# Output product of the first half moved up two slots in the first SAGE pass of a two-layer graph network

## The chip, the cores and the metric

The kernel runs on one core of a Trainium2 chip. The metric is the device time of one execution in microseconds; the time given for a kernel is the median over its runs. Engines of the core are written as in the profile: PE is TensorE (PEld its weight load), DVE is VectorE, ACT is ScalarE, POOL is GpSimd, SP is SyncE, which here only issues DMAs. Each engine works through its own instructions in the order in which the program gives them.

## The reference

Sixteen graphs of 1024 nodes with 128 channels go through two layers. Layer 0 is a gated graph network of four steps. Layer 1 thins out the adjacency row by row (`_dilate`), then runs three SAGE layers, each with a batch norm over all graphs, and a closing linear layer; each of the two layers ends with a residual sum and a layer norm. The part that matters here is the first SAGE layer:

```python
def _sage(x, adj, Wr, Wx, b, mf):
    deg = jnp.clip(jnp.sum(adj, axis=-1, keepdims=True), 1.0, None)
    agg = jnp.einsum('bij,bjd->bid', adj, x) / deg
    out = agg @ Wr + x @ Wx + b
    nrm = jnp.maximum(jnp.linalg.norm(out, axis=-1, keepdims=True), NORM_EPS)
    return out / nrm * mf[..., None]
...
h1 = _bn(jax.nn.relu(_sage(x, adj_d, Wr1, Wx1, b1, mf)), g1, be1)
h2 = _bn(jax.nn.relu(_sage(h1, adj_d, Wr2, Wx2, b2, mf)), g2, be2)
```

## The kernel before

The program has a stage for layer 0 and the thinning (up to about 1284 us of the profile), then `Sage.first` (to about 1747 us), `Sage.second`, `Sage.third` and `Sage.last`. The change lies in `Sage.first` alone.

`first` goes through the graphs b = -1 to 15, and through 16 slots t for each (`slot`, L1609). In a slot two things are interleaved: work on graph b (`now`), and preparation of the next graph n = b + 1 (`nxt`). The order in which `slot` issues instructions is the order on each engine; nothing is reordered by a scheduler there (`manual_schedule` over all engines).

Preparation of n: the transposed adjacency of the thinned graph is built in 16 units, one per slot. `unit` (L1482) issues four matmuls with the identity into a PSUM tile `p_u`, of which there are two, and an ACT instruction (L1495) for the part above the diagonal; `unit_low` (L1498) is one DVE instruction (L1503) for the part below it, and reads `p_u` too. `pack` (L1506) turns a finished unit into bytes on POOL a slot later. Units 3 to 7 have no ACT part, units 8 to 11 no DVE part. x of the next graph is normed (`norm_stats`, `norm`), turned by PE and copied by ACT into `p_xt0` and `p_xt1` (`turn_x`), and split into a high and a low part (`split_x`: ACT cast L1419, POOL subtraction L1420), `p_xh` and `p_xl`.

Work on b, with f = 0, 1 for the two halves of 512 nodes:

- the sum over neighbours: eight matmuls on `p_xh` (high sum) and eight on `p_xl` (low sum) into one PSUM bank, slots 0 and 1 for f = 0, slots 3 and 4 for f = 1 (`agg`, L1568);
- its copy to SBUF by ACT (`evict`, L1573, tile `s_ag`) at the head of slots 2 and 5, then the degrees (`degrees`: DVE L1556, ACT cast L1557 into `p_row`), whose columns PE turns in slots 3 and 6 (`degree_columns`, L1559; DVE L1565 and L1566);
- the output product (`out_first`, L1579): twelve matmuls into `p_oa` (aggregate by Wr) and `p_ob` (bias parts and x by Wx), each of one PSUM buffer;
- the chain of the half: `scale_rows` (DVE L1395, L1396), `squares` (ACT L1403 eight records, L1404), `rows` (DVE L1409 to L1414), `split_r` (ACT L1419, POOL L1420) into `p_rh` and `p_rl`;
- the neighbour sums of r for the second SAGE layer on `p_rh` and `p_rl` in slots 9, 10, 12 and 14, both halves of columns in one slot, and the turn of r in slots 11 and 13 (`turn_r`).

`check` (L1513) is a DVE instruction over a loaded block of the adjacency in slots 2, 5, 8, 10, 12 and 14. Between PE's instructions of one slot the order is: unit, sum, output product, degree columns, turn of r, sum of r, turn of x. In one slot, slot 6, `unit_low` is issued behind `scale_rows` rather than right after the unit.

SP's queue takes, in program order, the loads of the next adjacency blocks (`load_a`), of the thinning's result (`load_nr`) and of x, and the stores: bytes of the adjacency, the three rows of `rho` (L1690, slot 7), r (L1692), x (L1697), and in slot 1 the sums of r of the graph before (L1708), which frees the two buffers of `s_ag`. POOL issues no DMA in this pass.

In graph 0, the weights are prepared at the end of slot 3 (`first_weights`, L1306): it replaces the first row of `wr[:, 0, :]`, fills the bias rows `r6`, and fills the node mask.

Of the kernel before, what the change touches and what calls it, by code (L numbers as in the profile page):

```python
# [917 lines left out]
class Gated:  # L918
# [25 lines left out]
    def bank(self):  # L944
        return self.ps6.tile([P, HF], F32, name="h_g")
# [264 lines left out]
class Sage:  # L1210
# [398 lines left out]
    def slot(self, b, t):  # L1609

        nc, g, n = self.nc, self.g.get(b), b + 1
        now, nxt = b >= 0, n < B

        if nxt:
            if t in (4, 6):
                self.load_nr(n + 1, (t - 4) // 2)
            if t == 7:
                self.load_s(n + 1)
            if t in (10, 13):
                self.load_a(n, 2 + t // 13)  # L1620
        if now and t in (0, 2, 5, 8):
            self.load_a(b, (0, 2, 5, 8).index(t) + 4)

        if now:
            if t in (2, 5):
                g["ag", t // 5] = self.evict(g.pop(("pa", t // 5)), -1, 0)
            if t == 15:
                g["ag2"] = [self.evict(g.pop(("pb", f)), b, f) for f in range(2)]
        if nxt:
            self.unit(n, t)  # L1630
            if t != 6 or not now:
                self.unit_low(n, t)
            if t:
                self.pack(n, t - 1)
        if now and t == 0:
            self.pack(b, 15)
        if now:
            bank = lambda: self.ps3.tile([C, HF], F32, name="p_ag")
            if t in (2, 5):
                self.degrees(b, t // 5)  # L1640
            if t in (0, 1, 3, 4):
                f, lo = t // 3, t in (1, 4)
                if not lo:
                    g["pa", f] = bank()
                self.agg(g["pa", f], (self.xh, self.xl)[lo], g["at"], f, range(NB), not lo, lo)
            if t in (5, 7):
                self.out_first(b, t // 7)
            if t in (6, 8):
                f = t // 8
                g["o", f] = self.scale_rows(b, f, g.pop(("oa", f)), g.pop(("ob", f)))  # L1650
                if t == 6 and nxt:
                    self.unit_low(n, t)
            if t in (3, 6):
                pt = bank() if t == 6 else self.ps1.tile([P, 4, P], F32, name="s_tr").rearrange("p a b -> p (a b)")
                self.degree_columns(b, t // 6, pt[:, :4])
            if t in (7, 9):
                f = t // 9
                g["r", f] = self.rows(b, f, g.pop(("o", f)), g.pop(("ss", f)))
            if t in (8, 10):
                self.split_r(b, t // 10)  # L1660
            if t in (6, 8):
                g["ss", t // 8] = self.squares(g["o", t // 8])
            if t in (11, 13):
                self.turn_r(0, b, t // 13, self.ps1)
            if t in (9, 10, 12, 14):
                part = g["rl"] if t in (10, 14) else g["rh"]
                js = range(4 * (t // 12), 4 * (t // 12) + 4)
                for f in range(2):
                    if t == 9:
                        g["pb", f] = bank()  # L1670
                    self.agg(g["pb", f], part, g["at"], f, js, t == 9, t == 14)

        if nxt:
            if t < 2:
                self.norm_stats(n, t)
            if t in (2, 3):
                self.norm(n, t - 2)
            if t in (6, 8):
                self.turn_x(n, t // 8)
            if t in (7, 12):  # L1680
                self.split_x(n, t // 12)
        if now and t in (2, 5, 8, 10, 12, 14):
            self.check(b, (2, 5, 8, 10, 12, 14).index(t) + 2)

        if now:
            if t == 2:
                nc.sync.dma_start(self.at8[b, 1], g["b", 1])
            if t == 7:
                for i in range(3):
                    nc.sync.dma_start(self.rho[b, i:i + 1, :], g["rho"])  # L1690
            if t in (13, 15):
                nc.sync.dma_start(self.rt[b, t // 15], g["rt", t // 15])  # L1692
        if nxt:
            if t == 10:
                nc.sync.dma_start(self.at8[n, 0], self.g[n]["b", 0])
            if t == 13:
                nc.sync.dma_start(self.x1[n], self.g[n]["s"])  # L1697
        if (b, t) == (-1, 11):
            self.load_given()
        if (b, t) == (-1, 15):  # L1700

            for i in range(3):
                nc.sync.dma_start(self.rho[:, 3 + i, :], self.mask48[:B, :])
        if (b, t) == (0, 3):
            self.first_weights()
        if t == 1 and b >= 1:
            for f in range(2):
                nc.sync.dma_start(self.ag[b - 1, f], self.g[b - 1]["ag2"][f])  # L1708
            del self.g[b - 1]
# [368 lines left out]
```

## Time and profile before

| what | value |
|---|---|
| median of 3 runs | 2189.92 us (2189.5 to 2190.53) |
| the profiled execution, whole | 2193.03 us |
| its span, first to last instruction | 2191.1 us |
| mean granted TensorE clock | 0.986 |
| first sum product of graph 1, of graph 15 | 1333.83 us, 1721.84 us |

The busy shares, engine by engine, hold for the whole span, over stages that have different limits. For this change the stretch of the 14 graphs between the last two times is what is to be read; one graph looks like the next there. The stretch by windows (busy us of each engine, number of instructions, granted clock, busy share of the DMA engines, GB/s):

```profile
1333.83:1721.84 388.01, 361.94 (x2688) 293.31 (x2686) 342.81 (x869) 251.97 (x715) 284.13 (x281) 1.00 0.86 297
```

The engines in that line are PE, PEld, DVE, ACT, POOL. In a timeline line the columns are the start, the time taken, the engine, the line, the operation, the tiles written and read, the shapes, how many instructions are merged, and in brackets the idle time just before with what ended it. A matmul of fp32 operands has two records, so eight records are four matmuls. The time taken of a group of matmuls is longer than the distance to the next group, since they are pipelined.

### The profile page before, as it was taken

How to read it: one execution, taken by the hardware profiler on the slowest of the kernel's cores; microseconds unless marked ns; L12 is line 12 of the kernel's file. 1: busy time of each engine (PE TensorE's matmuls, PEld its weight loads, DVE VectorE, ACT ScalarE, POOL GpSimd, SP SyncE). 2: the span in 40 equal slices, each digit the busy share in tenths (PEclk: the TensorE clock that was granted, in tenths of full speed). 3: DMA queues.
4: the chain of work that ended last, by engine and by line, in shares of the span. 5: the costliest groups of instructions: out<-in, count | busy, mean ns of one | idle time of the engine just before them, and what ended most of it. 6: DMA issues, size and time to landing. Idle time of an engine off the chain costs nothing. (4 is left out here: it accounts for less than half of the span.)

```text
span 2191.1 us, 32979 instructions
## 1 busy us (share of the span) xinstructions
PE 2068.8 (94%) x10217; PEld 1441.4 (66%) x10217; DVE 1838.4 (84%) x4215; ACT 1326.7 (61%) x3238; POOL 1240.4 (57%) x1226
## 2 busy tenths in 40 slices
PE   6999999999999999999999979999999899998977
PEld 4666556666556665556665557777777678887866
DVE  4898998989998889988989978888888767766878
ACT  3657557565666656656575566666666445555757
POOL 4458558467566476575585447777777445551002
PEclk9999999999999999999999989999999999999989
DMA  8348446456455276474383259888888577765505
GB/s 256 76 96 252 90 121 224 86 154 192 92 177 166 77 205 146 97 226 109 83 261 92 68 200 334 306 301 304 302 306 298 178 268 264 268 230 175 156 21 156
DMA packets 233853, 406.13 MB, mean 185 GB/s; under 512 B 79042, under 2 KB 100196, under 8 KB 233668
## 3 DMA queue, kind: packets, MB, share of 16 engines
q1 hardware_dynamic: 187844, 284.37, 39.9%
q0 software_dynamic: 41472, 117.46, 20.2%
q10 hardware_dynamic: 4352, 2.11, 0.4%
q8 instruction: 83, 1.36, 0.3%
q14 instruction: 102, 0.84, 0.1%
HBM read 313.48 MB, written 109.25 MB: 193 GB/s over the span
## 5 line engine op out<-in xcount | busy, mean ns | idle before, releaser
L1104 PE MATMUL h_g<-h_h,h_wh 128*128 128x512 f32 x768 | 396.0, 597 | 3.3 <-DVE h_r L1116 3.3
L1104 PE MATMUL h_g<-h_ms,h_wi 128*128 128x512 f32 x768 | 392.2, 592 | 0.0
L1123 POOL TENSOR_TENSOR h_zh<-h_r,h_h 128x512 f32<-128x512 f32 x126 | 175.4, 1392 | 258.9 <-ACT h_r L1119 255.8
L737 DVE TENSOR_TENSOR_SCAN f_rank<-f_a,f_first,f_pd 128x1024 f16<-128x1024 bf16 x128 | 299.4, 2345 | 4.2
L1092 PE MATMUL h_g<-h_a,h_hi 128*128 128x512 f32 x1024 | 278.8, 413 | 1.3 <-DMA h_a<-in_adj_dram 1.2
L1104 PEld LDWEIGHTS h_g<-h_ms,h_wi 128*128 128x128 f32 x768 | 145.5, 190 | 184.3 <-issue 169.4
L1511 POOL CAST p_b<-p_at 128x512 uint8<-128x512 f32 x256 | 219.7, 880 | 82.8 <-DVE p_at L1503 52.3
L1092 PE MATMUL h_g<-h_a,h_lo 128*128 128x512 f32 x1024 | 262.0, 393 | 0.2 <-DVE h_lo L1030 0.2
L1092 PEld LDWEIGHTS h_g<-h_a,h_hi 128*128 128x128 f32 x1024 | 190.1, 188 | 62.2 <-issue 21.8
L1403 ACT ACTIVATE s_junk<-s_o 128x128 bf16<-128x128 f32 x384 | 114.0, 298 | 169.2 <-DVE s_o L1396 158.3
L1092 PEld LDWEIGHTS h_g<-h_a,h_lo 128*128 128x128 f32 x1024 | 189.7, 188 | 39.0 <-DVE h_lo L1030 1.0
L1104 PEld LDWEIGHTS h_g<-h_h,h_wh 128*128 128x128 f32 x768 | 133.3, 190 | 100.3 <-issue 73.4
L1125 POOL TENSOR_TENSOR h_h<-h_h,h_zh 128x512 f32<-128x512 f32 x126 | 179.0, 1420 | 9.9
L1119 ACT ACTIVATE h_r<-h_r,h_bi 128x512 f32<-128x512 f32 x128 | 92.4, 722 | 151.5 <-DVE h_r L1118 151.4
L1124 POOL TENSOR_TENSOR h_zh<-h_z,h_zh 128x512 f32<-128x512 f32 x126 | 162.5, 1290 | 9.9
L1095 ACT COPY h_ms<-h_g 128x512 f32<-128x512 f32 x128 | 73.9, 577 | 149.7 <-PE h_g L1092 149.6
L910 ACT ACTIVATE f_u<-f_rank,f_q 128x128 f16<-128x128 f16 (+7 forms) x128 | 110.6, 867 | 69.4 <-DVE f_rank L850 69.4
L1778 PE MATMUL q_ob<-s_wxp,q_xt 128*128 128x256 f32 x512 | 125.3, 389 | 3.5 <-DVE s_ss L1409 2.1
L1992 DVE SCALAR_TENSOR_TENSOR p_junk<-p_a 128x1024 bf16<-128x1024 f32 x96 | 126.0, 1312 | 0.0
L887 ACT ACTIVATE f_pd<-f_rank,f_q 128x128 f32<-128x128 f16 x128 | 59.1, 462 | 98.7 <-DVE f_q L701 95.5
L1503 DVE SCALAR_TENSOR_TENSOR p_at<-p_nr,p_u 128x128 fp32r<-128x128 bf16 (+1 forms) x192 | 102.0, 543 | 18.0 <-ACT p_at L1495 14.6
L778 POOL TENSOR_SCALAR_AFFINE_SELECT f_both<-f_both 128x512 bf16<-128x512 bf16 x32 | 20.5, 642 | 165.1 <-DVE f_both L777 165.1
(264 smaller groups left out, 4807.8 us busy)
## 6 DMA issues: line engine op xcount, KB each, us to landing
h_a<-in_adj_dram POOLq DMA_DIRECT2D x128, 512.0 KB, 9.2
p_a<-in_adj_dram SPq DMA_DIRECT2D x96, 512.0 KB
f_a<-in_adj_dram POOLq DMA_DIRECT2D x128, 256.0 KB, 6.5
e_nr<-f_nr SPq DMA_DIRECT2D x128, 256.0 KB
p_nr<-e_nr SPq DMA_DIRECT2D x32, 1024.0 KB
h_test<-in_adj_dram SPq DMA_DIRECT2D x32, 512.0 KB
s_at<-p_b SPq DMA_DIRECT2D x32, 512.0 KB
s_ag<-s_ag SPq DMA_DIRECT2D x64, 256.0 KB
```

The costliest lines, as they stand in the source:

```text
L737: nc.vector.tensor_tensor_scan(out, a, other[:, 0, 0:1].to_broadcast([P, N]), start, op0=ALU.add, op1=ALU.bypass)
L910: nc.scalar.activation(u[:, :n1], rank[:, g, :n1], AF.Abs, bias=q[:, 1, g:g + 1], scale=q[:, 0, g:g + 1])
L1092: nc.tensor.matmul(pm[f], part[:, j, :], st.adj[j][:, half[f]], start=(j == 0 and n == 0), stop=(j == NB - 1 and n == 1))
L1104: nc.tensor.matmul(pg, lhs, rhs, start=(i == 0), stop=(i == len(mm) - 1))
L1123: aid.tensor_tensor(d, r, h, ALU.subtract)
L1124: aid.tensor_tensor(d, z, d, ALU.mult)
L1125: aid.tensor_tensor(h, h, d, ALU.add)
L1403: self.nc.scalar.activation(junk, o[:, i, :], AF.Square, accum_out=ss[:, i:i + 1])
L1503: self.nc.vector.scalar_tensor_tensor(g["at"][:, j, c0:c0 + low], v[:, j, c0:c0 + low], 0.0, pu[:, :low], op0=ALU.is_lt, op1=ALU.is_lt)
L1511: self.nc.gpsimd.tensor_copy(g["b", f][:, j, :], g["at"][:, j, f * HF:(f + 1) * HF].bitcast(F32))
L1778: nc.tensor.matmul(pb[:, i], g["xt"][:, f, blk], self.wxp, start=(i % 2 == 0), stop=False)
L1992: nc.vector.scalar_tensor_tensor(junk, a, 0.0, a, op0=ALU.is_gt, op1=ALU.not_equal, accum_out=bad[:, c:c + 1])
```

## The change

The output product of half 0 goes to slot 3, and the high sum of half 1 to slot 2, so the product stands between the high and the low sum of half 1. The chain of half 0 follows (`scale_rows` and `squares` in slot 4, `rows` in 6, `split_r` in 7). The output product of half 1 goes to slot 6, its `scale_rows` and `squares` to slot 7. `rows` and `split_r` of half 1 stay in 9 and 10. `turn_x` of half 0 goes to slot 5, `split_x` of half 0 to slot 8. `unit_low` is issued behind `scale_rows` in slots 4 and 7, no longer in slot 6. `first_weights` stays at the end of slot 3 of graph 0.

```diff
-            if t != 6 or not now:
+            if t not in (4, 7) or not now:
                 self.unit_low(n, t)
...
-            if t in (0, 1, 3, 4):
-                f, lo = t // 3, t in (1, 4)
+            if t in (0, 1, 2, 4):
+                f, lo = t // 2 if t < 4 else 1, t in (1, 4)
                 if not lo:
                     g["pa", f] = bank()
                 self.agg(g["pa", f], (self.xh, self.xl)[lo], g["at"], f, range(NB), not lo, lo)
-            if t in (5, 7):
-                self.out_first(b, t // 7)
-            if t in (6, 8):
-                f = t // 8
+            if t in (3, 6):
+                self.out_first(b, t // 6)
+            if t in (4, 7):
+                f = t // 7
                 g["o", f] = self.scale_rows(b, f, g.pop(("oa", f)), g.pop(("ob", f)))
-                if t == 6 and nxt:
+                if nxt:
                     self.unit_low(n, t)
...
-            if t in (7, 9):
+            if t in (6, 9):
                 f = t // 9
                 g["r", f] = self.rows(b, f, g.pop(("o", f)), g.pop(("ss", f)))
-            if t in (8, 10):
+            if t in (7, 10):
                 self.split_r(b, t // 10)
-            if t in (6, 8):
-                g["ss", t // 8] = self.squares(g["o", t // 8])
+            if t in (4, 7):
+                g["ss", t // 7] = self.squares(g["o", t // 7])
...
-            if t in (6, 8):
+            if t in (5, 8):
                 self.turn_x(n, t // 8)
-            if t in (7, 12):
+            if t in (8, 12):
                 self.split_x(n, t // 12)
```

## The prediction

> **What bounds the kernel now.** I read the share of busy time first, then the waits of the first SAGE pass (1290 to 1730 us), then one graph of it engine by engine in the timeline, then the granted clock by windows. The page's chain of waits names only the last ACT instruction, so the chain is followed by hand.
>
> ```profile
> PE 2068.8 (94%) x10217; PEld 1441.4 (66%) x10217; DVE 1838.4 (84%) x4215; ACT 1326.7 (61%) x3238; POOL 1240.4 (57%) x1226
> ```
>
> PE is busiest, but DVE is close behind. In the pass itself, from 1333.83 to 1721.84 us, PE is busy 361.94 and DVE 342.81 of 388.01 us. Those two times are the starts of the first product on p_xh in graphs 1 and 15, so a graph takes 388.01 / 14 = 27.72 us. PE's waits there, by their sums over 15 graphs:
>
> ```profile
> PE p_ag L1570 <- POOL p_rl L1420: 12.5, 15, 0.9
> PE p_ag L1570 <- ACT p_rh L1419: 11.7, 15, 1.1
> PE s_tr L1425 <- ACT p_xt L1548: 3.6, 15, 0.3
> ```
>
> Three waits, once per graph each, 27.8 us together. Below is graph 10, whose slot 0 product starts at 1583.22 us; I call this 0 and give later times from it. First PE, then DVE, then ACT:
>
> ```profile
> 1589.96 2.09 PE L1570 MATMUL p_ag<-p_at,p_xl 128*128 128x512 f32 x8
> 1591.90 0.40 PE L1490 MATMUL p_u<-ident_b,p_nr 128*128 128x128 bf16 x4
> 1592.13 1.11 PE L1585 MATMUL p_oa<-s_wr,s_ag 128*128 128x128 f32 x8
> 1594.25 0.39 PE L1490 MATMUL p_u<-ident_b,p_nr 128*128 128x128 bf16 x4
> ...
> 1599.62 2.14 PE L1570 MATMUL p_ag<-p_at,p_rh 128*128 128x512 f32 x8 [0.76 <-ACT p_rh L1419]
> 1601.60 0.40 PE L1490 MATMUL p_u<-ident_b,p_nr 128*128 128x128 bf16 x4
> 1602.80 2.12 PE L1570 MATMUL p_ag<-p_at,p_rl 128*128 128x512 f32 x8 [0.81 <-POOL p_rl L1420]
> ```
>
> ```profile
> 1594.43 0.67 DVE L1395 TENSOR_TENSOR s_o<-p_oa,s_rdeg 128x512 f32<-128x512 f32 x1
> 1595.21 0.69 DVE L1396 TENSOR_TENSOR s_o<-p_ob,s_o 128x512 f32<-128x512 f32 x1
> 1595.82 0.68 DVE L1503 SCALAR_TENSOR_TENSOR p_at<-p_nr,p_u 128x512 fp32r<-128x512 bf16 x1
> 1596.41 0.15 DVE L1565 TENSOR_SCALAR s_rdeg<-p_ag 128x4 f32<-128x4 f32 x1
> ```
>
> ```profile
> 1592.35 0.56 ACT L1576 COPY s_ag<-p_ag 128x512 f32<-128x512 f32 x1
> 1592.94 0.62 ACT L1557 CAST p_row<-s_ag 1x512 f16<-1x512 f32 x1
> 1595.93 0.31 ACT L1403 ACTIVATE s_junk<-s_o 128x128 bf16<-128x128 f32 x1 [2.37 <-DVE s_o L1396]
> ```
>
> The reader is to see two regimes. From slot 10 to slot 4 PE runs without a wait and sets the pace. From slot 5 to slot 10 DVE runs from one instruction straight into the next, and PE waits for what hangs on it: the cast of r (16.40) and its remainder (19.58).
>
> **The change part by part.** Nothing is added or removed; the same instructions stand in another order. On PE the first half's output product (twelve matmuls, 24 records, 2.12 us from 1592.13 to 1594.25) goes from slot 5 to slot 3, the second half's high sum from slot 3 to 2, the second output product from 7 to 6, the first turn of x from 6 to 5. On DVE, scaling, deferred low part and norm of half 0 go two and one slots up, those of half 1 one slot, except rows(1), which stays. On ACT the nine squares of half 0 go from slot 6 to 4, **ahead of the copy of the second half's sum (L1576, slot 5)**. The split of x goes a slot down (ACT 0.62, POOL 1.47), that of r one up (ACT 0.62, POOL 2.24). No DMA issue moves; the rho stores follow degrees(1), about 2.9 us later, and behind them on SP's queue stands a p_a load that is checked six slots later, so I cost that at nothing (if that slack were gone, check(14) on DVE would wait).
>
> PE, with the row distances of graph 10: slot 2's unit 4.07, second high sum 4.28, unit 3 at 6.21 (+1.93), output product 0 at 6.44. Its sum is copied by 5.47 (1588.10 + 0.59), so no wait. Degree columns 8.56 to 8.80, unit 4, low sum 8.88 to 10.81, unit 5, turn of x, unit 6; ready for output product 1 at 11.73.
>
> DVE: reciprocal degrees 8.85, scaling at 9.13 (+0.28). Squares on ACT start 1.50 later (1594.43 to 1595.93): 10.63. They hold ACT for 1.43 (1595.93 to 1597.36), and only then comes the copy of the second sum: 12.06 to 12.62. So output product 1 starts at 12.67, **a new PE wait of 0.94**. Behind it on PE stand the degree columns and units 7 and 8; DVE's degrees(1) also waits for this copy, and check(5), the low part of unit 6 and rows(0) stand behind that.
>
> From there the chain is DVE's: degrees 0.35 + check 1.14 + low part 0.59 from 12.66 ends at 14.74; PE's product and degree columns end at 15.02, so reciprocal degrees 15.07, rows(0) 15.35, scaling(1) 16.64 (1.29, 1597.48 to 1598.77), low part of unit 7 at 18.04 (1.40), done 18.71. Unit 9 uses unit 7's PSUM buffer (two of them), so PE, idle since its turn of x ended at about 15.97, waits until 18.76: **2.79 us, a second new wait**. The r sums stand behind it: high at 18.97, low at 21.16 without a wait, because the remainder is there by about 19.6. In graph 10 that low sum starts at 19.58. From it to the next graph PE leads, so the remaining 8.01 stays and the graph takes 29.17 us: 1.45 over the mean, times 14 = 20.3 us.
>
> The first graph issues its first output product ahead of the weight preparation (first_weights, end of slot 3), so there it reads weights and bias parts before they are prepared: that changes what is computed for that graph's first 512 rows, and lets PE fill part of the 2.0 us in which it waited on that preparation; I take +1.2 for it. The last graph has no units; the squares still delay the second sum there, about +1.0 by the same distances. **Sum of order alone: 22.5 us.** POOL's subtraction overlapping DVE can add: a check that takes 1.21 took 1.45 beside it, up to 0.3 per graph, 4 us.
>
> **The clock.** A PE wait of 2.8 us is new to this pass. Windows of 3.41 us, with PE's busy time and the granted clock:
>
> ```profile
> 1307.48:1310.90 3.42, 2.10 (x13) 1.00 0.85 211
> 1310.90:1314.31 3.41, 3.41 (x15) 0.50 1.04 305
> 1764.87:1768.28 3.41, 1.68 (x12) 1.00 0.39 85
> 1768.28:1771.69 3.41, 2.98 (x14) 1.00 0.89 316
> 2109.62:2113.03 3.41, 0.66 (x4) 1.00 0.00 0
> 2113.03:2116.44 3.41, 1.12 (x4) 0.50 0.00 0
> ```
>
> Half clock follows the windows with 0.66 and 2.10 us busy, not the one with 1.68. So busy time alone does not decide; but a window that holds all of the new wait is busy 0.62, next to the row of 0.66. Price of one slow window: in graph 0 the low sum took 3.26 (1310.03 to 1313.29) against 2.17 and the next product's first part 1.44 against 0.95, together 1.58. Ends: no graph, 0; all fourteen, 22.1. With the boundary midway between 0.66 and 1.68 (1.17) a window must hold 2.24 of the 2.79; that is so for 0.62 + 2 x 0.55 = 1.72 of 3.41 positions, half. Nine windows are 30.72, almost 29.17 + 1.58, so a graph that falls in passes its position on to the next. I take 8 of 14: 12.6 us.
>
> The Trainium skill speaks against this term: "TensorE: Matmul & The Clock Gate", section "Why this matters for your kernels", sees a drop only from PE-idle gaps over about 3 us. By it a 2.79 us wait keeps the full clock and the time would be about 2212. The row at 1307.48 differs: the longest gap there is 1.35 us and the clock fell.
>
> **Sum.** Against the profiled execution: span 2191.1 + 22.5 + 12.6 = 2226.2 (whole 2193.03 + 35.1 = 2228.1). That execution was 3.1 over the median of the runs, 2189.92, so the forecast for the median is 2225.
>
> **Rivals.** Order without clock: 2189.9 + 22.5 = 2212; for it, no idle stretch exceeds 2.8 and may be cut in two by a window's edge. Faster: the r chain is earlier, PE's waits 0.20 + 0.76 + 0.81 = 1.77 vanish and nothing takes their place, 14 x 1.77 = 25, 2165; for it, they are PE's largest waits; against it, DVE would have to finish the low part of unit 7 by about 15.4, and decides from there on. No net change, 2190: the new waits would have to total just the 1.77. Slower by the copy of the first sum: its buffer is freed by a store, and in the last graph that copy waited 4.84 us; its product was 3.4 us away and is now 1.0, each us beyond costs one; in the fourteen graphs it waits at most 0.70, so I see at most 14 more, 2239.
>
> **How the numbers follow.** Chances: forecast (order and clock) 0.48, order alone 0.34, faster 0.07, no change 0.05, late store 0.06. The range 2205 to 2237 holds the first two: below, order at 1.1 per graph; above, the clock in all graphs. Slower by over 0.2% (some 4 us, about what a measurement can tell) 0.88, same 0.05, faster 0.07.
>
> **What would show it.** In the profile after: PE's output product 1 waiting for ACT's copy (about 0.9), unit 9 on PE waiting for DVE L1503 (2 to 3 us), no wait for POOL p_rl, graphs of 29.2 us at full clock and 30.7 with a half-clock window. Wrong would be graphs under 27.7, or no wait ahead of unit 9: then DVE has more slack than its gapless rows show.

## The result, and the profile after

The changed kernel takes 2240.32 us (2239.49 to 2240.92) against 2190.23 us beside it: a ratio of 1.0225, 95% interval 1.0212 to 1.0238. It is slower, as forecast, but by 50 us and not by 35, and 3 us above the range. The profiled execution has a span of 2237.7 us, 46.6 more than before. The two profiles lie 3 us less far apart than the medians.

The stretch of graphs 1 to 14 again, by windows (busy PE, PEld, DVE, ACT, POOL, granted clock, DMA share, GB/s). The first product on p_xh of graph 15 now starts at 1763.82 us:

```profile
1334.45:1763.82 429.37, 378.60 (x2688) 306.30 (x2686) 348.75 (x869) 250.21 (x715) 278.57 (x283) 0.94 0.80 269
```

It took 388.01 us and takes 429.37: a graph went from 27.72 to 30.67 us. ACT is busy for as long as before (250.21 against 251.97 us), DVE for 6 us more; the mean clock in the stretch fell from 1.00 to 0.94. Of the 46.6 us, 41.4 are here, 0.6 before graph 1 and 4.6 behind the start of graph 15 (469.26 to 473.90). PE's waits in the stretch, all of them that the view lists, changed kernel:

```profile
PE p_u L1490 <- DVE p_at L1503: 38.3, 14, 2.7
PE p_oa L1585 <- ACT s_ag L1576: 12.5, 14, 0.9
```

The three waits shown of before (27.8 us over 15 graphs) are gone. In their place stand two new ones, 50.8 us over 14. Graph 10, which starts at 1610.62 us, timeline of PE and then of DVE and ACT:

```profile
1623.37 1.16 PE L1585 MATMUL p_oa<-s_wr,s_ag 128*128 128x128 f32 x8 [0.90 <-ACT s_ag L1576]
...
1629.42 0.38 PE L1490 MATMUL p_u<-ident_b,p_nr 128*128 128x128 bf16 x4 [2.73 <-DVE p_at L1503]
1629.61 3.38 PE L1570 MATMUL p_ag<-p_at,p_rh 128*128 128x512 f32 x8
1632.80 0.65 PE L1490 MATMUL p_u<-ident_b,p_nr 128*128 128x128 bf16 x4
1633.20 2.25 PE L1570 MATMUL p_ag<-p_at,p_rl 128*128 128x512 f32 x8
```

```profile
1623.35 0.41 DVE L1556 TENSOR_SCALAR p_rho<-s_ag 1x512 bf16<-1x512 f32 x1 [0.82 <-ACT s_ag L1576]
...
1628.69 0.68 DVE L1503 SCALAR_TENSOR_TENSOR p_at<-p_nr,p_u 128x512 fp32r<-128x512 bf16 x1
```

```profile
1622.63 0.21 ACT L1404 ACTIVATE s_ss<-s_ss 128x4 f32<-128x4 f32 x1
1622.74 0.57 ACT L1576 COPY s_ag<-p_ag 128x512 f32<-128x512 f32 x1
```

From the graph's start, output product 1 is at 12.75 (predicted 12.67), the low part of unit 7 at 18.07 (18.04), unit 9 at 18.80 (18.76), the high sum at 18.99 (18.97). Then the high sum, 2.14 us before, takes 3.38. The windows of the clock for graphs 9, 10 and 11 and for the last graph (us, PE busy, granted clock, DMA share, GB/s):

```profile
1595.92:1599.34 3.42, 0.69 (x7) 1.00 0.31 125
1599.34:1602.75 3.41, 3.41 (x13) 0.50 0.42 83
1626.64:1630.06 3.42, 0.69 (x7) 1.00 0.39 144
1630.06:1633.47 3.41, 3.41 (x13) 0.50 0.52 100
1657.36:1660.78 3.42, 0.69 (x7) 1.00 0.31 123
1660.78:1664.19 3.41, 3.41 (x13) 0.50 0.46 95
...
1773.42:1776.83 3.41, 1.41 (x13) 1.00 0.01 3
1776.83:1780.24 3.41, 2.11 (x15) 0.50 0.49 155
```

Each graph has one window with about 0.7 us of PE busy (0.68 to 0.77) and then one at half clock, and these stand 30.72 us apart, nine windows, in all fourteen graphs. In the last graph the clock is halved for three windows, 10.2 us. PE's waits there:

```profile
1775.62 1.16 PE L1585 MATMUL p_oa<-s_wr,s_ag 128*128 128x128 f32 x8 [2.00 <-ACT s_ag L1576]
...
1781.37 3.78 PE L1570 MATMUL p_ag<-p_at,p_rh 128*128 128x512 f32 x8 [2.43 <-ACT p_rh L1419]
```

### The profile page after: what moved, and what is told of

Its sections match the earlier page's. It is cut to its first block, busy times and chain, and to the rows that moved or that the text cites. A ratio compares the mean times of both kernels' runs of the same rounds, so it can differ in the third digit from the quotient of the medians.

```text
span 2237.7 us, 32963 instructions
## 1 busy us (share of the span) xinstructions
PE 2089.3 (93%) x10217; PEld 1458.3 (65%) x10217; DVE 1844.0 (82%) x4215; ACT 1324.7 (59%) x3238; POOL 1231.0 (55%) x1226
## 5 line engine op out<-in xcount | busy, mean ns | idle before, releaser
L1490 PE MATMUL p_u<-ident_b,p_nr 128*128 128x128 bf16 x1024 | 100.6, 229 | 50.3 <-DVE p_at L1503 47.9
L1992 DVE SCALAR_TENSOR_TENSOR p_junk<-p_a 128x1024 bf16<-128x1024 f32 x96 | 143.3, 1492 | 0.0
L1490 PEld LDWEIGHTS <-p_nr 128*128 128x128 bf16 x1024 | 68.0, 102 | 91.4 <-issue 90.6
L1495 ACT ACTIVATE p_at<-p_u 128x512 fp32r<-128x512 f32 (+3 forms) x160 | 75.1, 472 | 73.5 <-PE p_u L1490 72.8
```

The costliest lines, as they stand in the source:

```text
L1490: nc.tensor.matmul(pu[:, i * P:(i + 1) * P], v[:, 4 * f + i, j * P:(j + 1) * P], self.cst["ident_b"], start=True, stop=True)
L1992: nc.vector.scalar_tensor_tensor(junk, a, 0.0, a, op0=ALU.is_gt, op1=ALU.not_equal, accum_out=bad[:, c:c + 1])
```

## The experiments

All are timed in several rounds, but for the two with few filling matmuls, which have one execution each. Graph lengths are means over graphs 1 to 14 of the profiled execution.

**Fill the wait.** Is it the clock that makes the sums on r slow, or something else?

```diff
-                    if t == 9:
+                    if t == 9 and f:
                         g["pb", f] = bank()
...
+        if now and t == 8:
+            g["pb", 0] = bank()
+            for i in range(12):
+                nc.tensor.matmul(g["pb", 0], self.cst["ident_b"], self.mask48[:, :HF], start=True, stop=True)
```

> The changed kernel, with 12 extra bf16 matmuls (128x128 by 128x512) on PE at the end of slot 8, behind the turn of x and ahead of unit 9, into the bank that slot 9 overwrites: they fill the 2.73 us in which PE waits for the low part of unit 7 and change no result. Theory (half clock follows the idle window): no half-clock window in graphs 1 to 14, a graph takes 29.2 us instead of 30.7, time 2214 to 2222. Rival (the sums on p_rh are slow for another reason, for instance operands contended by POOL and ACT): the high sum still takes 3.4 us, a graph 30.7 or more, time 2238 or more.

Measured: 2220.45 us, ratio 1.0137 (1.0117 to 1.0156); the profiled execution took 2216.39. No half-clock window in graphs 1 to 14, a graph 29.30 us. The stretch of these graphs, and the PE timeline of the graph that starts at 1568.47:

```profile
1334.06:1744.21 410.15, 394.51 (x2856) 309.04 (x2854) 359.00 (x869) 249.27 (x715) 276.67 (x281) 1.00 0.83 281
```

```profile
1584.58 2.75 PE L1685 MATMUL p_ag<-s_mask,ident_b 128*128 128x512 bf16 x12
1587.48 0.38 PE L1490 MATMUL p_u<-ident_b,p_nr 128*128 128x128 bf16 x4
1587.67 2.07 PE L1570 MATMUL p_ag<-p_at,p_rh 128*128 128x512 f32 x8
```

PE does 2.75 us more work per graph and the graph is 1.37 us shorter; the high sum is back at 2.07. The theory stands, the rival falls. Unit 9 is at 19.01 here and at 18.79 in most graphs of the changed kernel. The filling is not the reason: with four fillings (below), behind which PE still waits 1.88 us for DVE, unit 9 stands at 19.0 too in graphs that follow one at full clock, and at 18.8 in those that follow a slow one. So 29.30 is the order alone. Behind the start of graph 15 this run takes 469.99 against 473.90: the filling, which is there too, takes away most of what the last graph lost. The profiled execution is the fastest of the four; the others took 2218.75 to 2223.35 us, at a mean clock of 0.983 to 0.985 where this one has 0.987. So they were at half clock for longer, and no trace shows where.

**Where the clock falls.** The same with 2 and with 4 filling matmuls:

```diff
-            for i in range(12):
+            for i in range(2):
```

> The changed kernel with 2 filling matmuls of the first experiment (0.43 us) instead of 12: the emptiest window has then about 0.33 of PE busy instead of 0.20. Theory (half clock follows a window with PE busy for less than about a third): at the boundary, half clock in at least half of graphs 1 to 14, 2226 to 2240. Rival (only windows busy a fifth or less, the lowest rows of the kernel before): no half-clock window, 2214 to 2220.

> The same with 4 filling matmuls (0.85 us): the emptiest window busy about 0.45. Theory: no half-clock window in graphs 1 to 14, a graph 29.3 us, 2214 to 2222. Rival (idle stretches of about 1.3 us are enough, as in graph 0 of the kernel before): half clock in most graphs, 2230 or more.

Measured: with 2, 2238.4 us, half clock in 13 of the 14 graphs; with 4, 2230.81 us, half clock in 7 of 14 (those take 30.5 to 30.9 us, the others 29.1 to 29.3, but for one of 30.7 at full clock, which is followed below). First a pair of windows with 2 fillings, then three pairs with 4:

```profile
1443.62:1447.03 3.41, 1.05 (x8) 1.00 0.43 165
1447.03:1450.45 3.42, 3.42 (x12) 0.50 0.47 91
```

```profile
1470.75:1474.16 3.41, 1.48 (x12) 1.00 0.53 180
1474.16:1477.57 3.41, 3.41 (x21) 1.00 0.31 46
1501.47:1504.88 3.41, 1.53 (x10) 1.00 0.22 85
1504.88:1508.30 3.42, 3.42 (x12) 0.50 0.66 181
1562.91:1566.32 3.41, 1.53 (x11) 1.00 0.11 43
1566.32:1569.74 3.42, 3.42 (x24) 1.00 0.70 182
```

With 1.05 us busy the clock falls; at about 1.5 it does so in some windows and not in others with the same busy time. The expectation for 2 fillings held, that for 4 did not: the boundary lies at about 1.5 of 3.41 us by this measure of busy, not at a third. In graphs 1 to 14 of all the runs here, half clock follows every window with 1.40 us or less, and none with 1.56 or more. The time with 4 is the rival's (2230 or more), its reason is not: waits of 1.4 to 1.6 us stand in every graph of three kernels below, without a half-clock window in graphs 1 to 14.

The long graph at full clock is graph 2. ACT and PE in it:

```profile
1372.90 0.59 ACT L1576 COPY s_ag<-p_ag 128x512 f32<-128x512 f32 x1 [2.04 <-DMA s_ag<-s_ag]
```

```profile
1373.54 1.16 PE L1585 MATMUL p_oa<-s_wr,s_ag 128*128 128x128 f32 x8 [0.94 <-ACT s_ag L1576]
```

The copy of the first sum waited for the store that frees its buffer, and the output product, now close behind, waited for the copy. This is the late store that the prediction gave a chance of 0.06. In graphs 1 to 14 of the changed kernel's profile it did not occur.

**Take the waits away one at a time.** The low part of unit 7 ahead of the scaling:

```diff
-            if t not in (4, 7) or not now:
+            if t != 4 or not now:
                 self.unit_low(n, t)
...
-                if nxt:
+                if t == 4 and nxt:
                     self.unit_low(n, t)
```

> The changed kernel, with the low part of unit 7 issued right behind the unit again, ahead of the scaling of half 1 (only slot 4's stays deferred). Theory (unit 9 waits for that one DVE instruction, and the idle time it makes costs the clock): unit 9 released 1.4 us earlier, idle 1.3 us, no half clock, a graph about 27.8 us, time 2190 to 2197. Rival (DVE as a whole is the bound in slots 5 to 10, so what is put first only shifts the wait): a graph 28.5 us or more, time 2203 or more.

Measured: 2222.31 us, 1.0138 (1.0117 to 1.016). The half clock is gone from the graphs, but a graph takes 29.45 us, not 27.8, and so no less than in the filled run: the time is as the rival had it. PE timeline of graph 10:

```profile
1618.23 0.38 PE L1490 MATMUL p_u<-ident_b,p_nr 128*128 128x128 bf16 x4 [1.42 <-DVE p_at L1503]
1618.42 2.08 PE L1570 MATMUL p_ag<-p_at,p_rh 128*128 128x512 f32 x8
1621.60 0.38 PE L1490 MATMUL p_u<-ident_b,p_nr 128*128 128x128 bf16 x4 [1.09 <-ACT p_at L1495]
```

Unit 9's wait fell from 2.73 to 1.42, as expected. But unit 10 now waits 1.09 us for the ACT part of unit 8, which stands behind the squares of half 1 on ACT. Behind unit 9's long wait it had not shown.

The copy of the second sum ahead of the squares:

```diff
-            if t in (2, 5):
-                g["ag", t // 5] = self.evict(g.pop(("pa", t // 5)), -1, 0)
+            if t == 2:
+                g["ag", 0] = self.evict(g.pop(("pa", 0)), -1, 0)
...
+            if t == 4:
+                g["ag", 1] = self.evict(g.pop(("pa", 1)), -1, 0)
             if t in (4, 7):
                 g["ss", t // 7] = self.squares(g["o", t // 7])
```

> The changed kernel, with ACT's copy of the second sum issued in slot 4 ahead of the squares of half 0. Theory (the squares hold the copy and so the second output product by 0.9 us): product 1 starts at about 11.75 instead of 12.74 with no wait for the copy; unit 9 still waits some 2.7 us; a graph 28.25 us at full clock, 29.8 with a half-clock window; since 28.25 and 29.8 are not whole numbers of 3.41 us windows, only part of the graphs lose the clock; time 2200 to 2215. Rival (product 1 waits for something else): no change, 2240.

Measured: 2215.36 us, 1.0112 (1.0094 to 1.013). Output product 1 starts without a wait, at 11.69 in graph 10:

```profile
1605.36 1.11 PE L1585 MATMUL p_oa<-s_wr,s_ag 128*128 128x128 f32 x8
```

Graphs of 28.17 and 29.93 us take turns, with half clock in every second one: the two together are 58.1 us, seventeen windows of 3.413. The lengths are within 0.13 us of those expected, and the time is 0.4 us above the expected 2200 to 2215; the squares do hold the copy. Unit 9 waits 2.90 us here, a little more than in the changed kernel.

Both edits, and graph 0's weight preparation first:

```diff
-        if (b, t) == (0, 3):
+        if (b, t) == (0, 2):
             self.first_weights()
```

> Both of the former edits together, and the weight preparation of graph 0 moved from the end of slot 3 to the end of slot 2, ahead of the first output product that reads it. Theory: product 1 at 11.75, rows of half 0 done by 15.7, unit 9 and the high sum at about 16.6, low sum at 18.9 where the kernel before has 19.6: a graph 27.0 to 27.2 us, time 2178 to 2188, under the kernel before. Rival (DVE's total work bounds the graph): 27.7 us or more, 2190 or more.

Measured: 2204.09 us, 1.0061 (1.0043 to 1.0079), a graph 28.52 us without a half clock. Unit 9 goes at 16.94 (expected 16.6), and then unit 10 waits 1.09 us again. The time is the rival's, its reason is not shown: DVE is busy 344.11 of the 399.25 us of the 14 graphs, and PE waits for single instructions of DVE and ACT.

**Follow the waits.** The squares of half 1 a slot later:

```diff
-            if t in (4, 7):
-                g["ss", t // 7] = self.squares(g["o", t // 7])
+            if t in (4, 8):
+                g["ss", t // 8] = self.squares(g["o", t // 8])
```

> The kernel of the last run, with the squares of half 1 issued on ACT in slot 8, behind the ACT part of unit 8, instead of in slot 7. Theory (what took the place of the removed waits is unit 10 on PE, 1.09 us per graph, which uses the buffer of unit 8, whose ACT part stands behind those squares): that wait vanishes, low sum on r at about 19.3, a graph 27.3 to 27.6 us, time 2184 to 2192. Rival (DVE's total work bounds the graph): 28.2 us or more, 2198 or more.

Measured: 2204.86 us, 1.0065 (1.0048 to 1.0081), a graph 28.63 us. PE's waits in graphs 1 to 14:

```profile
PE p_u L1490 <- DVE p_at L1503: 22.1, 14, 1.6
PE p_ag L1570 <- POOL p_rl L1420: 18.7, 14, 1.4
```

Unit 10's wait is gone, and 1.34 us per graph of waiting for POOL's remainder of r (half 1) has come. The time is the same, as the rival had it.

Rows and checks moved on DVE:

```diff
+            if t == 6:
+                g["r", 0] = self.rows(b, 0, g.pop(("o", 0)), g.pop(("ss", 0)))
             if t in (3, 6):
                 pt = bank() if t == 6 else ...
...
-        if now and t in (2, 5, 8, 10, 12, 14):
-            self.check(b, (2, 5, 8, 10, 12, 14).index(t) + 2)
+        if now and t in (2, 7, 9, 10, 12, 14):
+            self.check(b, (2, 7, 9, 10, 12, 14).index(t) + 2)
```

> As the former, and on DVE the rows of half 0 ahead of the reciprocal degrees of half 1, check(5) moved to slot 7 and check(8) to slot 9. Theory (the chain on DVE from the second sum's degrees to the low part of unit 7 sets when unit 9 goes; DVE idles 1.7 us later in the graph, so the checks can stand there): rows done by 14.8, unit 9 at about 15.8, high sum on r at 16.0, a graph 26.2 to 26.9 us, time 2170 to 2182. Rival (DVE's total work bounds the graph at what the former run shows): no change against it.

Measured: 2205.67 us, 1.0064 (1.0047 to 1.0081), a graph 28.66 us. No change against the former, as the rival says. DVE's check is the same instruction in both kernels; here is its group (mean ns of one after the bar) before and in this run, same stretch:

```profile
L1992 DVE SCALAR_TENSOR_TENSOR p_junk<-p_a 128x1024 bf16<-128x1024 f32 x81 | 106.0, 1309 | 0.0
```

```profile
L1995 DVE SCALAR_TENSOR_TENSOR p_junk<-p_a 128x1024 bf16<-128x1024 f32 x79 | 140.2, 1775 | 0.4
```

A check takes 1775 ns where it took 1309: 2.7 us more per graph over the six of them with their short reads (11.01 against 8.31), of which 1.6 are left in DVE's busy time of a graph (24.5 before, 26.1 here). The instruction was not edited. In the run with the later squares, from which this one differs only by the moves shown, it takes 1468. The traces show what stands beside the long ones: the 41 checks that overlap POOL's subtraction (L1420) take 2.13 us on the mean and the other 42 take 1.44; in the filled run it is 1.88 (56 checks) and 1.21 (28). In the kernel before the two kinds hardly differ (1.33 and 1.30), and the overlap was not tried by itself, so it is not shown to be the cause.

**Parts of the change alone, on the kernel before.** The split of x a slot later, then also the turn of x a slot earlier:

```diff
-            if t in (6, 8):
+            if t in (5, 8):
                 self.turn_x(n, t // 8)
-            if t in (7, 12):
+            if t in (8, 12):
                 self.split_x(n, t // 12)
```

> The kernel before with one part of the change alone: the split of x of half 0 in slot 8 instead of 7. Theory (the change carried a gain of its own: POOL's remainder of r no longer stands behind that of x, so PE's wait of 0.83 us ahead of the low sum on r vanishes, and the loss is the order of output product, copy and squares): low sum at about 18.7 instead of 19.6, a graph 26.9 to 27.2 us, time 2178 to 2184. Rival (what one POOL instruction frees turns up as a wait elsewhere, as in the former runs): a graph 27.6 us or more, 2188 or more.

> As the former, and the turn of x of half 0 in slot 5 instead of 6, as the change has it too. Theory: PE's wait of 0.24 us for the turn of half 1 vanishes as well, a graph 26.7 to 27.0 us, time 2175 to 2182. Rival: no change against the former.

Measured: 2202.34 us, 1.0051 (1.0035 to 1.0068), and 2200.5 us, 1.0051 (1.0034 to 1.0069). Both miss with the wrong sign. PE's waits in the first of them:

```profile
PE p_ag L1570 <- ACT p_rh L1419: 17.3, 15, 1.5
PE p_ag L1570 <- POOL p_rl L1420: 15.9, 13, 1.2
```

The wait of 0.83 us for the remainder of half 0 is gone, but POOL's remainder of x now stands ahead of the remainder of r of half 1, which comes 1.23 us too late in slot 14. PE's wait for the cast of r has grown as well, from 0.79 to about 1.16 us in most graphs. So this part alone costs 12 us (8 to 15 by the interval). In the second run the wait for the turn is gone, as expected, and the wait for the cast takes its place (23.5 us in all). In the changed kernel's waits the remainder does not show, since PE is late there already; the next run tests whether it is what PE waited for in the run with the later squares.

**Mend both.** The split of x in slot 6 in the first of the next two kernels (on the one with the later squares), in slot 5 in the second (on the kernel before):

```diff
-            if t in (8, 12):
+            if t in (6, 12):
                 self.split_x(n, t // 12)
```

```diff
-            if t in (7, 12):
+            if t in (5, 12):
                 self.split_x(n, t // 12)
```

> The kernel with the copy first, the low part of unit 7 first and the squares of half 1 in slot 8, and the split of x of half 0 in slot 6 instead of the change's 8. Theory (POOL's remainder of x, issued late, holds back the remainder of r of half 1, 1.34 us per graph on PE; earlier it stands in a gap of POOL of 2 us): that wait vanishes, a graph 27.2 to 27.5 us, time 2182 to 2190, so the product in slot 3 is then worth nothing or a little. Rival (another wait again): 28.2 us or more, 2198 or more.

> The kernel before with the split of x of half 0 in slot 5 instead of 7: the opposite of the change's move. Theory (the place of POOL's remainder of x decides which remainder of r is late; at slot 5 it stands in ACT's and POOL's gap before the squares): PE's wait of 0.83 us ahead of the low sum on r vanishes and none takes its place, a graph 26.8 to 27.1 us, time 2176 to 2182, faster than both kernels. Rival: no change against the kernel before, 2188 to 2192, or slower.

Measured: the first 2206.07 us, 1.0071 (1.005 to 1.0092). POOL's wait is gone, so it was that, and unit 9 waits 2.55 us for DVE again, so graphs of 27.87 us at full clock mostly take turns with graphs of about 29.9 (half clock in 6 of 14). Even the full-clock ones are no shorter than the 27.72 before. The second: 2187.56 us, 0.9984 (0.9975 to 0.9994), a graph 27.50 us. It is the fastest version of this study, by 0.16%, with a graph 0.2 us shorter where 0.6 to 0.9 were expected: POOL's wait is gone, but the wait for ACT's cast of r grew from 0.79 to 1.19 us.

## Why the prediction missed

The direction and the chain were right. Predicted and measured, in us:

| term of the sum | predicted | measured | from |
|---|---|---|---|
| order, graphs 1 to 14 | 20.3 | 22.1 | filled run, 410.15 - 388.01 |
| half clock, graphs 1 to 14 | 12.6 | 19.2 | 429.37 - 410.15 |
| first graph | 1.2 | 0.6 | start of graph 1 |
| last graph, order | 1.0 | 0.7 | filled run, 469.99 - 469.26 |
| last graph, half clock | none | 3.9 | 473.90 - 469.99 |
| sum (span) | 35.1 | 46.6 | |

The measured terms come from one profiled execution of each kernel. Over the runs of this study the start of graph 1 lies between 1331.3 and 1336.7 us, and the part behind the start of graph 15 takes 467.9 to 473.9, so the terms of the first and the last graph are known to a few microseconds only. Forecast and measurement lie 15.3 us apart by the medians (2225 and 2240.32) and 11.8 by the profiled executions (2228.1 and 2239.92): the prediction took off 3.1 us because the execution profiled before lay that much above its median, and the one profiled after lies 0.4 below its own.

- **The two new waits** were placed and sized right: 0.94 predicted and 0.90 found ahead of output product 1, 2.79 and 2.73 ahead of unit 9. Moving the copy ahead of the squares took the first away; issuing unit 7's low part earlier shortened the second by the 1.3 us that this makes. The filled run shows the order separately from the clock: 29.30 us per graph, 29.17 predicted.
- **The step that failed** is the count, "I take 8 of 14"; the runs showed 14 of 14, and 19.2 us of half clock in place of 12.6. I took the share of window positions that fall in (1.72 of 3.41) as the share of the graphs. The sentence ahead of it should have stopped me: a slow graph is almost nine windows long, so it hands its position on, and one that has fallen in stays in. A graph that stays out is 29.17 us by my own sum, 1.55 short of nine windows, and the positions that are out were only 1.69 wide: it falls in after one such graph, seldom two. So the same figures give 12 to 14 graphs. The run with 2 fillings shows it: graph 1 stays at full clock (29.23 us), and then all thirteen that follow are slow. The boundary was wrong too: 1.17, "midway between 0.66 and 1.68", where the runs put it at about 1.5. The trace of before has one row between the two, a window with 1.50 us busy at 822.79 us that kept the clock, so it could not have told. But this did not decide: the windows that cost the clock in the changed kernel are busy for 0.68 to 0.77 us, under either value.
- **The price of a slow window**, 1.58 predicted, was right inside a graph: with four fillings a slow graph takes 30.69 us, and the next, at full clock and behind a slow graph as it was, 29.11. A graph behind a slow one is 0.2 us shorter than one behind a graph at full clock (29.31), so a chain of slow graphs pays 1.37 each. All fourteen at 1.58 would have made the forecast 2234.5, inside the range, which had been drawn to hold just this case.
- **The last graph's clock** was not in the sum at all. Its wait of 2.00 us ahead of output product 1 leaves a window with 1.41 us busy, and half clock follows. The wait of 2.43 us ahead of the first sum on r falls into that slow stretch, which lasts three windows. Without these 3.9 us, as far as two profiles tell, the time would have been just inside the range.
- **The clock's limit.** 2.73 us of idle PE was enough in every graph, and windows with some 1.9 us free were enough in part; waits of 1.4 to 1.6 us cost no window in graphs 1 to 14. The Trainium skill ("TensorE: Matmul & The Clock Gate", "Why this matters for your kernels") names gaps of about 3 us; here the measurement decides, and it is less.
- **The split of x**, which the prediction left without a price, costs 12 us by itself; within the change no wait for it shows, since a longer one stands ahead of it.
- **The rivals.** Order without clock was 2212; the filled run comes near that case, at 2216 in its profiled execution and 2220 by its median. PE's three old waits vanished as the faster rival said, and did not help, because DVE's chain came behind them. The late store did not occur in the profile of the changed kernel, but it did in other kernels with the product in slot 3: in one graph with 4 fillings, which took 1.4 us more by it, and in five graphs of the run with the moved rows, whose first output product waited 0.4 to 0.9 us.

Not settled: graph 0's half clock in the kernel before follows a window with 2.10 us busy, above the boundary found, and in graph 0 of three other runs it follows windows with 1.59 to 1.65. Which activity beyond the profile's busy time is counted, no run here tells.

## What to carry to other kernels

Moving a product up one engine's queue moves what hangs on it ahead of others' work on every other queue: list for each engine what the moved instructions now stand in front of, and follow the last of those to the engine that bounds. A new wait of 2.5 to 3 us on PE in a loop like this one must be priced twice, as idle time and as a slow window after it, and if the slowed loop comes close to a whole number of windows, price it in every turn. A share of positions is not a share of turns when each turn hands its position to the next. Where several chains end within a microsecond of each other, taking one wait away shows the next one: in four edits of this study it was of about the size of the one removed, in a fifth half of it.

## What the runs showed of the hardware that was not expected

The clock windows and the loop lock together: with half clock in each graph the period is 30.67 us (nine windows are 30.72); with half clock in every second graph it is 58.1 (seventeen are 58.0). Extra matmuls made the kernel faster, 2220.45 against 2240.32 us: twelve kept the clock in graphs 1 to 14 of the profiled execution, four, which leave windows with about 1.5 us busy, in half of them, and two, which leave 1.05, in one. A DVE instruction that was not edited went from 1468 to 1775 ns on the mean when others and two of its own six places in a graph were moved.
